# A convolution-attention layer followed by attention and experts: V projected behind the positional products, x loaded late, Q's first half in a written order

## Chip, core and metric

The kernel runs on one core of one Trainium2 chip, in one launch. The metric is the device time of the whole launch in microseconds (us), as the median of several runs. All arrays are float32. PE is TensorE (its weight loads are PEld), DVE is VectorE, ACT is ScalarE, POOL is GpSimd; SP is SyncE, from whose queue most transfers (DMAs) are issued.

## What is computed

The input x is 4 x 16 x 16 x 1024: 1024 positions ("tokens") in 4 images, 1024 channels. Layer 0 is the one that the change touches; cut to what matters it is

```python
xn = group_norm(x)                       # 32 groups of 32 channels, per image
q = bn(xn @ Wq, gamma, beta, mean, var)  # 1024 columns, 4 heads of 256
k = softmax(xn @ Wk)                     # 256 columns
v = bn(xn @ Wv, ...)                     # 256 columns
Lc = einsum("bkm,bvm->bkv", k, v)        # content
Yc = einsum("bhkn,bkv->bnhv", q, Lc)
Lp = einsum("nmk,bvm->bnkv", rel, v)     # relative positions
Yp = einsum("bhkn,bnkv->bnhv", q, Lp)
x = x + Yc + Yp
```

where bn(t) = (t - mean) * gamma / sqrt(var + 0.001) + beta. Layer 1, which the change leaves alone, is layer norm, multi-head attention with its projection, a second layer norm and eight gated experts, all added to x.

## The kernel before, in words

All tiles have 128 partitions. A float32 matmul runs as two passes, which the profile counts as two instructions. PSUM is held as eight banks: three under the tag mm, three under tr, and one tile of two banks under sc. The order of instructions on each engine, and of transfers on each queue, is not the program's order: a planner places an instruction when its inputs are ready in the planner's own picture of time, the earlier in the program first. Each engine and each queue then works strictly in that order, and an instruction whose semaphores are not there yet holds up those behind it.

**Loads (lines 178 to 209).** The tile xn receives x transposed, one chunk of 128 channels after the other, alternating with chunks of the first half of Wq; then come the second half of Wq, the four batch-norm rows of Q (tile q_rows), the positional table emb and, last, the eight tiles xs of x in its own layout (line 209). x is needed only where the result of layer 0 is added to it (line 429). Two large places called big0 and big1 (32 KB per partition each) are used in turn by many tiles: xn and then s0 use big0; q_rows, two_T and ln1 use big1. The eight xs tiles have a pool of their own. The two places of wpool hold, in turn, the two halves of Wq, w_kv, ln_rows and the two halves of w_v.

**Group norm and Q's first half (lines 214 to 295).** For each chunk c, group_means takes statistics on DVE and averages them over groups with a small matmul (pm); group_spreads does it for the variance (pv, line 233); group_norm takes the inverse root and lets ACT normalise the chunk in place, in four pieces. Six of the eight token tiles of Q's first half (the list early) are multiplied chunk by chunk as the chunks become ready, in six banks; the norms run two chunks ahead. batch_norms prepares scale and shift of V (vp) and Q (q_scale, q_shift); its reciprocal over 1024 columns is line 131, called from line 257. q_out (line 266) scales a bank into q_s (line 268), which frees the bank, and spreads it over q0 with four additions (line 272). The other ten token tiles follow one at a time in mm banks.

**K and V (lines 303 to 345).** K is projected and put through its softmax; then V in four groups of eight matmuls, each copied to v_T by ACT (line 339).

**Positional products (lines 366 to 402).** s0[m, n] sums, for every position n and head, what multiplies v at position m. The positional part is built in four groups R, with matmuls pT of windows of emb (copied by POOL, line 382, four buffers) and q0. The results of a group go to a half of two_T by ACT and DVE in turn (line 392). When a group is complete, its rows are moved to their partitions of s0 by transfers on SP's queue (line 399), 60 in all: 23, 22, 8 and 7 for R = 1, 2, 0 and 3. R = 0 reuses the half of R = 1, and R = 3 that of R = 2.

**Content and result (lines 347 and 410 to 432).** For each of eight token tiles, content adds the products of K and Q to s0 (line 361); the matmuls py multiply s0 by v_T (line 422); DVE adds the result to xs (line 429); layer_norm makes ln1 for layer 1; and x plus a bias is stored to x_rows (line 432), from which layer 1 reads it back at line 656.

Of the kernel before, what the change touches and what calls it, by code (L numbers as in the profile page):

```python
# [31 lines left out]
F32 = mybir.dt.float32  # L32
I32 = mybir.dt.int32
AF = mybir.ActivationFunctionType
ALU = mybir.AluOpType
# [3 lines left out]
P = 128  # L39
C = 1024  # L40
NC = C // P
B = 4
M = 256
TOK = B * M
NT = TOK // P
# [9 lines left out]
HALF = 512  # L55
BN_EPS = 0.001
# [9 lines left out]
def kernel(  # L66
# [27 lines left out]
    nc = tc.nc  # L94

    def pool(stack, name, bufs=1, **kw):
        return stack.enter_context(tc.tile_pool(name=name, bufs=bufs, reuse_waits="tile", **kw))
# [10 lines left out]
    def big_tile(n, name, shape=(NC, TOK)):  # L108
        return big[n].tile([P, *shape], F32, tag="big", name=name)
# [11 lines left out]
    def mm(name):  # L121
        return ps.tile([P, HALF], F32, tag="mm", name=name)
# [4 lines left out]
    def inverse_root(dst, var, eps):  # L127

        nc.vector.tensor_scalar(dst, var, eps, None, ALU.add)
        nc.scalar.activation(dst, dst, AF.Sqrt)  # L130
        nc.vector.reciprocal(dst, dst)
# [2 lines left out]
    make_identity(nc, ident)  # L134
    x_home = ExitStack()

    def tiles_of_x(name):
        xpool = pool(x_home, name, side="right")
        return [xpool.tile([P, C], F32, tag=f"x{t}", name=f"{name}{t}") for t in range(NT)]

    xs = tiles_of_x("x")
    dram = ctx.enter_context(tc.tile_pool(name="dram", bufs=1, space=bass.MemoryType.DRAM))
    x_rows = dram.tile([TOK, C], F32, name="x_rows")

# [30 lines left out]

    with ExitStack() as layer0:
        l0 = pool(layer0, "l0")
        xn = big_tile(0, "xn")
        w_q = [wpool.tile([P, NC, HALF], F32, tag="w", name=f"w_q{kc}") for kc in range(2)]
        for c in range(NC):  # L180
            nc.sync.dma_start(xn[:, c, :], xT[ts(c, P), :])
# [11 lines left out]
        with ExitStack() as projection:  # L193
# [8 lines left out]

            q_rows = big_tile(1, "q_rows", (NC, TOK))
            q_scale, q_shift, mean_q, var_q = (q_rows[:, i, :] for i in range(4))
            for t, a in ((q_scale, q_gamma), (q_shift, q_beta), (mean_q, q_mean), (var_q, q_var)):
                nc.sync.dma_start(t, a.partition_broadcast(P))
            nc.sync.dma_start(emb.rearrange("p c i j -> p c (i j)"), embT)
            for t in range(NT):
                nc.sync.dma_start(xs[t], x[ts(t, P), :])


            chunks = {}
# [1 line left out]
            def group_means(c):  # L214
                stats = small.tile([P, B, 6], F32, tag="gn_stats", name=f"gn_stats{c}")
                mv = small.tile([P, B, 2], F32, tag="gn_mv", name=f"gn_mv{c}")
                for b in range(B):
                    nc.vector.bn_stats(stats[:, b, :], xn[:, c, ts(b, M)])
                    nc.vector.bn_aggr(mv[:, b, :], stats[:, b, :])
                pm = tr(f"gn_pm{c}")  # L220
                nc.tensor.matmul(pm[:, :B], average, mv[:, :, 0], start=True, stop=True)
                chunks[c] = mv, pm
# [27 lines left out]


            def batch_norms():
                inverse_root(vp[:, 3, :], vp[:, 3, :], BN_EPS)
                nc.vector.tensor_mul(vp[:, 0, :], vp[:, 0, :], vp[:, 3, :])
                nc.vector.tensor_mul(vp[:, 2, :], vp[:, 2, :], vp[:, 0, :])
                nc.vector.tensor_sub(vp[:, 1, :], vp[:, 1, :], vp[:, 2, :])
                inverse_root(var_q, var_q, BN_EPS)
                nc.vector.tensor_mul(q_scale, q_scale, var_q)
                nc.vector.tensor_mul(mean_q, mean_q, q_scale)
                nc.vector.tensor_sub(q_shift, q_shift, mean_q)  # L260


            def q_product(pq, kc, t, c):
                nc.tensor.matmul(pq, xn[:, c, ts(t, P)], w_q[kc][:, c, :], start=(c == 0), stop=(c == NC - 1))  # L264
# [12 lines left out]

            two = ps.tile([P, 2, HALF], F32, tag="sc", name="pq_two", bufs=1)
            early = [mm(f"pq0_{t}") for t in range(3)] + [two[:, 0, :], two[:, 1, :], tr("pq0_5")]
            group_means(0)  # L280
            group_spreads(0)
            group_norm(0)
            group_means(1)
            group_spreads(1)
            group_norm(1)
            for c in range(NC):
                for t, pq in enumerate(early):
                    if c + 2 < NC and t in (1, 3):
                        (group_means if t == 1 else group_spreads)(c + 2)
                        if t == 3:  # L290
                            group_norm(c + 2)
                    q_product(pq, 0, t, c)
            batch_norms()
            for t, pq in enumerate(early):
                q_out(pq, 0, t)
            for kc in range(2):
# [27 lines left out]
                nc.vector.reciprocal(total, total)  # L324
                nc.vector.tensor_scalar(k_q[:, b, kc, :], k_e, total, None, ALU.mult)


            for j in range(2):
                for th in range(2):
                    pv = mm(f"pv{j}_{th}")  # L330
                    for c in range(NC):
                        nc.tensor.matmul(  # L332
                            pv,
                            w_kv[:, c, M + j * P : M + (j + 1) * P],
                            xn[:, c, ts(th, HALF)],
                            start=(c == 0),
                            stop=(c == NC - 1),
                        )
                    nc.scalar.activation(
                        v_T[:, j, ts(th, HALF)],  # L340
                        pv,
                        AF.Identity,
                        bias=vp[:, 1, j : j + 1],
                        scale=vp[:, 0, j : j + 1],
                    )

        def content(b, ih):

            heads = slice(b * HEADS0, b * HEADS0 + HEADS0)
# [17 lines left out]
        s0 = big_tile(0, "s0", (2, SIDE, SIDE, BH))  # L367
        tpool = pool(layer0, "tpool", 2)
        two_T = big_tile(1, "two_T", (2, SIDE, SIDE, BH))
        for n, (R, first, n_i) in enumerate(((1, 0, 16), (2, 0, 15), (0, 8, 8), (3, 0, 7))):  # L370
            rows = min(S2, REL - S2 * R)
            parts = rows * SIDE
            group = 2 if n_i > S2 else 4
            T = two_T[:, n % 2, :n_i, :, :]
            for n0 in range(0, SIDE, group):
                pT = mm(f"pT{R}_{n0}")
                out_T = pT[:parts, : group * BH * n_i].rearrange("p (j i h) -> p j i h", j=group, h=BH)
                for g in range(group):
                    nj = n0 + g
                    at = SIDE - 1 - nj  # L380
                    window = tpool.tile([P, 2, rows, SIDE], F32, tag="window", name=f"window{R}_{nj}", bufs=4, padded_shape=[P, 2, S2, SIDE])
                    nc.gpsimd.tensor_copy(window, emb[:, :, S2 * R : S2 * R + rows, at : at + SIDE])
                    for kc in range(2):
                        nc.tensor.matmul(
                            out_T[:, g, :, :],
                            window[:, kc, :, :].rearrange("p i j -> p (i j)"),
                            q0[:, kc, first : first + n_i, nj, :],
                            start=(kc == 0),
                            stop=(kc == 1),
                        )  # L390
                evict = nc.scalar.copy if n0 // group % 2 == 0 else nc.vector.tensor_copy
                evict(T[:parts, :, n0 : n0 + group, :].rearrange("p i j h -> p j i h"), out_T)
            for i in range(n_i):
                ni = first + i
                start = S2 * R + ni - SIDE + 1
                for mh in range(2):
                    lo, hi = max(start, mh * S2), min(start + rows, mh * S2 + S2)
                    if lo < hi:
                        nc.sync.dma_start(  # L399
                            s0[(lo - mh * S2) * SIDE : (hi - mh * S2) * SIDE, mh, ni, :, :],  # L400
                            T[(lo - start) * SIDE : (hi - start) * SIDE, i, :, :],
                        )

        ln1 = big_tile(1, "ln1")
        ln_rows = wpool.tile([P, 4, C], F32, tag="w", name="ln_rows")
        bp = ln_rows[:, 3, :]
        nc.gpsimd.dma_start(bp, b_proj.partition_broadcast(P))
        tiles = [(b, nt) for nt in (1, 0) for b in range(B)]  # L410
        for i, (b, nt) in enumerate(tiles):
            if i == 0:
                content(b, nt)
# [22 lines left out]
    with ExitStack() as attention:  # L436
# [212 lines left out]
        for i in range(len(steps) + 2):  # L649
            if i >= 2:  # L650
                s_T = turned(*steps[i - 2], soft.pop(i - 2))
            for unit in units.get(i, ()):
                project_qk(*unit)
            if i == 27:
                sums.close()
                xs = tiles_of_x("xb")
                for t in range(NT):
                    nc.sync.dma_start(xs[t], x_rows[ts(t, P), :])
            if i in out_at:
                project_out(*out_at[i])  # L660
            if i >= 2:
                values(*steps[i - 2], s_T)
            if i < len(steps):
                soft[i] = scores(*steps[i])
# [599 lines left out]
```

## Time and profile before

| what | value |
|---|---|
| median of 3 runs | 1316.14 us (1314.88 to 1316.62) |
| the profiled execution | 1314.95 us, of which the span from the first to the last instruction is 1313.2 us |
| mean granted PE clock | 0.996 |

Layer 0 by stretches, in us from the start of the span, with each engine's busy time:

| stretch | what PE works on | length | PE | DVE | ACT | POOL |
|---|---|---|---|---|---|---|
| 0 to 12.2 | first norms | 12.2 | 2.32 | 6.00 | 2.23 | 3.08 |
| 12.2 to 61.2 | Q, six early tiles | 49.0 | 47.41 | 29.87 | 19.71 | 0 |
| 61.2 to 129.9 | Q, the other ten | 68.7 | 68.70 | 41.15 | 0 | 0 |
| 129.9 to 157.8 | K | 27.9 | 27.90 | 9.67 | 3.96 | 1.97 |
| 157.8 to 185.4 | V | 27.6 | 27.60 | 0.94 | 2.90 | 0 |
| 185.4 to 230.5 | positional products | 45.1 | 41.89 | 7.40 | 8.78 | 23.76 |
| 230.5 to 303.7 | content, py, layer norm | 73.2 | 70.42 | 43.38 | 20.40 | 20.59 |
| 303.7 to 1313.2 | layer 1 | 1009.5 | 994.39 | 520.74 | 187.06 | 294.18 |

How to read the views. A line of the timeline gives start, duration, engine, source line, operation, the tile written and read, shapes and the number of merged instructions; in brackets stands how long the engine had been idle and what released it. A line of waits gives the waiting instruction, the one it waited for, the total, the number and the longest. PE's busy time includes matmuls that run at a lower granted clock, so slow matmuls are seen in the clock column and not as idle time.

### The profile page before, as it was taken

What the parts mean: (1) busy time and instruction counts of PE and PEld (TensorE: products, weight loads), DVE (VectorE), ACT (ScalarE), POOL (GpSimd) and SP (SyncE); (2) the same over time, 40 slices, a digit from 0 to 9 for tenths busy, and PEclk for the clock granted to TensorE, in tenths of its full rate; (3) what the DMA queues carried; (4) which work ended last, traced back from release to release, by engine and by line L of the source; (5) the groups of instructions that cost most, each with busy time, mean ns of one, the idle gap of its engine ahead of it and who ended that gap; (6) DMA issues with size and microseconds to landing.
All of it is one profiled execution on the core that took longest, in us unless ns stands there. A gap on an engine that the chain in (4) does not pass through costs nothing.

```text
span 1313.2 us, 12226 instructions
## 1 busy us (share of the span) xinstructions
PE 1280.6 (98%) x4506; PEld 690.6 (53%) x4506; DVE 659.1 (50%) x1248; ACT 245.0 (19%) x572; POOL 343.6 (26%) x365
## 2 busy tenths in 40 slices
PE   6999999999999999999999998999999999999998
PEld 3444858678884555555544544444444444444443
DVE  5674201567322555554435755664646465555642
ACT  3200111131000333333323322111111111111110
POOL 0000015131000111112111112455454544453530
PEclk9999999999999999999999998999999999999999
DMA  9320013212102202010405315284747566555542
GB/s 354 124 65 0 17 64 95 67 65 96 64 1 64 65 0 65 1 64 1 179 14 178 128 65 190 64 240 104 221 116 196 143 167 175 146 163 141 113 80 50
DMA packets 61040, 136.11 MB, mean 104 GB/s; under 512 B 5904, under 2 KB 20256, under 8 KB 60976
## 3 DMA queue, kind: packets, MB, share of 16 engines
q1 hardware_dynamic: 47664, 94.32, 20.6%
q0 software_dynamic: 13312, 40.96, 14.2%
q8 instruction: 37, 0.61, 0.2%
q14 instruction: 27, 0.22, 0.1%
HBM read 97.51 MB, written 33.55 MB: 100 GB/s over the span
## 4 chain that ended last, share of the span: by engine, by line
PE 91%; SPq 3%; DVE 2%; POOL 1%; issue 1%; DMA 1%; ACT 0%; DVEq 0%; ACTq 0%; POOLq 0%
PE p L1073 28%; PE pqk L470 15%; PE po L627 8%; PE pq L264 8%; PE pv L470 7%; PE one_pe L717 6%; SPq L399 3%; PE py L422 2%; PE pk L312 2%; PE pv L332 2%; PE sc L554 2%; PE pst L598 2%; PE pa L608 2%; PE pc L353 2%; PE pq_two L264 1%; POOL w_e_xg L696 1%
## 5 line engine op out<-in xcount | busy, mean ns | idle before, releaser
L696 POOL DMA_INDIRECT w_e_xg<-rows,gather x152 | 160.3, 1054 | 69.5 <-issue 41.8
L1073 PE MATMUL p<-w_e,A 128*128 128x512 f32 x368 | 162.9, 592 | 1.8 <-DVE slot L934 1.8
L586 POOL TENSOR_TENSOR s<-s,total 128x256 f32<-128x256 f32 x64 | 51.6, 827 | 341.1 <-DVE total L583 341.1
L1073 PEld LDWEIGHTS p<-w_e,A 128*128 128x128 f32 x368 | 69.8, 190 | 89.4 <-issue 88.0
L627 PE MATMUL po<-w_p,y_T 128*128 128x512 f32 x256 | 116.1, 598 | 0.0
L1073 PE MATMUL p<-T,S 128*128 128x512 f32 x256 | 112.7, 592 | 0.0
L724 POOL DMA_INDIRECT out_dram<-y,add x32 | 58.8, 1838 | 204.5 <-ACT y L1079 134.8
L1079 ACT ACTIVATE y<-y,slot 128x512 f32<-128x512 f32 x64 | 46.2, 722 | 340.1 <-DVE y L1087 166.4
L264 PE MATMUL pq<-w_q,xn 128*128 128x512 f32 x224 | 102.1, 608 | 1.6 <-ACT xn L243 1.6
L470 PE MATMUL pqk<-ln,w_qk 128*128 128x512 f32 x192 | 85.0, 592 | 0.0
L717 PE MATMUL one_pe<-w_e,one 128*128 128x512 f32 x192 | 83.4, 592 | 0.0
L1073 PEld LDWEIGHTS p<-T,S 128*128 128x128 f32 x256 | 48.6, 190 | 60.8 <-issue 60.7
L627 PEld LDWEIGHTS po<-w_p,y_T 128*128 128x128 f32 x256 | 46.3, 190 | 49.1 <-issue 48.7
L264 PEld LDWEIGHTS pq<-w_q,xn 128*128 128x128 f32 x224 | 42.7, 194 | 52.0 <-issue 48.9
L706 DVE STREAM_TRANSPOSE A<-w_e_xg 128x1024 f32<-128x1024 f32 x32 | 39.7, 1241 | 42.7 <-DMA w_e_xg<-rows,gather 42.6
L717 PEld LDWEIGHTS one_pe<-w_e,one 128*128 128x128 f32 x192 | 36.5, 190 | 45.9 <-issue 45.9
L576 ACT ACTIVATE s<-s,top 128x256 f32<-128x256 f32 (+1 forms) x128 | 56.6, 443 | 17.7 <-DVE top L574 17.7
L470 PEld LDWEIGHTS pqk<-ln,w_qk 128*128 128x128 f32 x192 | 35.9, 190 | 42.1 <-issue 41.1
L470 PE MATMUL pqk<-T,S_qk 128*128 128x512 f32 x128 | 57.7, 593 | 0.0
L1073 PE MATMUL p<-w_e,S 128*128 128x512 f32 x128 | 57.5, 592 | 0.0
L1073 PE MATMUL p<-T,A 128*128 128x512 f32 x128 | 57.5, 592 | 0.0
L599 ACT COPY s_T<-pst 128x384 f32<-128x384 f32 x64 | 27.5, 481 | 157.9 <-PE pst L598 157.9
(253 smaller groups left out, 1784.8 us busy)
## 6 DMA issues: line engine op xcount, KB each, us to landing
w_e<-in_expert_w_dram SPq DMA_DIRECT2D x16, 2048.0 KB, 11.4
w_qk<-in_W_attnT_dram SPq DMA_DIRECT2D x8, 1024.0 KB, 6.4
xn<-in_xT_dram SPq DMA_DIRECT2D x8, 512.0 KB, 8.1
x<-in_x_dram SPq DMA_DIRECT2D x8, 512.0 KB, 11.3
w_v<-in_W_attnT_dram SPq DMA_DIRECT2D x2, 2048.0 KB, 8.2
x_rows<-x SPq DMA_DIRECT2D x8, 512.0 KB, 2.6
w_p<-in_W_projT_dram SPq DMA_DIRECT2D x2, 2048.0 KB, 7.6
xb<-x_rows SPq DMA_DIRECT2D x8, 512.0 KB, 7.6
```

Source lines behind the costliest of these rows:

```text
L264: nc.tensor.matmul(pq, xn[:, c, ts(t, P)], w_q[kc][:, c, :], start=(c == 0), stop=(c == NC - 1))
L399: nc.sync.dma_start(s0[(lo - mh * S2) * SIDE : (hi - mh * S2) * SIDE, mh, ni, :, :], T[(lo - start) * SIDE : (hi - start) * SIDE, i, :, :],)
L470: nc.tensor.matmul(bank, stationary(c), moving(c), start=(c == 0), stop=(c == NC // 2 - 1))
L576: nc.scalar.activation(s[:, h, cols], s[:, h, cols], AF.Exp, bias=top[:, qt, h : h + 1], accum_out=total[:, qt, h : h + 1],)
L586: nc.gpsimd.tensor_mul(s[:, :, cols], s[:, :, cols], total[:, qt, :].unsqueeze(2).to_broadcast([P, 2, (qt + 1) * P]),)
L627: nc.tensor.matmul(po, y_T[:, c, ts(t, P)], w_p[j][:, c, :], start=(c == 0), stop=(c == NC - 1))
L696: nc.gpsimd.indirect_dma_start(out=row[:, g, :], out_offset=None, in_=table[: (TOK - P) * Q, :] if e in SHORT else table, in_offset=bass.I ...
L706: nc.vector.transpose(row_T.rearrange("p c (g j) -> p g c j", g=Q), row.rearrange("p g (c i) -> p g c i", c=NC),)
L717: nc.tensor.matmul(pe, row_T[:, c, :], w[j][:, c, :], start=(c == 0), stop=(c == NC - 1))
L724: nc.gpsimd.indirect_dma_start(out=out[: TOK - P, :] if e in SHORT else out, out_offset=bass.IndirectOffsetOnAxis(ap=add[:, e, k : k + 1], ...
L1073: nc.tensor.matmul(bank, a[:, c, :], b[:, c, :], start=(c == 0), stop=(c == NC // 2 - 1))
L1079: nc.scalar.mul(y[i][:, ts(j, HALF)], y[i][:, ts(j, HALF)], slot[:, e, 1, 2 * pair + i : 2 * pair + i + 1])
```

## The change

1. **Places.** xn moves from big0 to a pool x_pool; s0 then has big0 to itself. x is no longer loaded at the start: a tile x_at of the same tag as xn, so in the same place, is loaded behind V's projection, in the order in which the tiles are used.
2. **V behind the positional products.** The loop of V's four groups stands behind the loop of the groups R and ahead of the loads of x.
3. **Places in two_T.** R = 3 writes rows 8 to 14 of the first half, so it reuses a part of what R = 1 held; R = 0 keeps rows 0 to 7 of it.
4. **Q's first half in a written order.** Within manual_schedule each engine issues its instructions in the order of the program; where they fall among instructions outside the block stays the planner's. The norms run one chunk ahead instead of two. keep_warm issues matmuls whose result is overwritten: 14 ahead of the first means, 3 and 5 in the steps behind. The inverse root of Q's variance is taken in pieces: root after chunk 4, a quarter of the reciprocal after chunks 5 and 6 each, the last half after the loop; Q's scale then stands ahead of V's in batch_norms. The row var_q is the first of the four to be loaded.

```diff
-    xs = tiles_of_x("x")
+    x_pool = pool(x_home, "x_pool", side="right")
...
-        xn = big_tile(0, "xn")
+        xn = x_pool.tile([P, NC, TOK], F32, tag="x", name="xn")
...
-            for t, a in ((q_scale, q_gamma), (q_shift, q_beta), (mean_q, q_mean), (var_q, q_var)):
+            for t, a in ((var_q, q_var), (q_scale, q_gamma), (mean_q, q_mean), (q_shift, q_beta)):
                 nc.sync.dma_start(t, a.partition_broadcast(P))
             nc.sync.dma_start(emb.rearrange("p c i j -> p c (i j)"), embT)
-            for t in range(NT):
-                nc.sync.dma_start(xs[t], x[ts(t, P), :])
...
             def batch_norms():
+                nc.vector.tensor_mul(q_scale, q_scale, var_q)
+                nc.vector.tensor_mul(mean_q, mean_q, q_scale)
+                nc.vector.tensor_sub(q_shift, q_shift, mean_q)
                 inverse_root(vp[:, 3, :], vp[:, 3, :], BN_EPS)
...
-                inverse_root(var_q, var_q, BN_EPS)
-                nc.vector.tensor_mul(q_scale, q_scale, var_q)
-                nc.vector.tensor_mul(mean_q, mean_q, q_scale)
-                nc.vector.tensor_sub(q_shift, q_shift, mean_q)
...
-            group_means(0)
-            group_spreads(0)
-            group_norm(0)
-            group_means(1)
-            group_spreads(1)
-            group_norm(1)
-            for c in range(NC):
-                for t, pq in enumerate(early):
-                    if c + 2 < NC and t in (1, 3):
-                        (group_means if t == 1 else group_spreads)(c + 2)
-                        if t == 3:
-                            group_norm(c + 2)
-                    q_product(pq, 0, t, c)
-            batch_norms()
+
+            def keep_warm(n):
+                for _ in range(n):
+                    nc.tensor.matmul(early[0][:, :P], average, average, start=True, stop=True)
+
+            with tc.manual_schedule():
+                keep_warm(14)
+                group_means(0)
+                keep_warm(3)
+                group_spreads(0)
+                keep_warm(5)
+                group_norm(0)
+                for c in range(NC):
+                    for t, pq in enumerate(early):
+                        q_product(pq, 0, t, c)
+                        if t == 1 and c + 1 < NC:
+                            group_means(c + 1)
+                        elif t == (3 if c == 0 else 2) and c + 1 < NC:
+                            group_spreads(c + 1)
+                            group_norm(c + 1)
+                    if c == NC - 4:
+                        nc.vector.tensor_scalar(var_q, var_q, BN_EPS, None, ALU.add)
+                        nc.scalar.activation(var_q, var_q, AF.Sqrt)
+                    elif NC - 4 < c < NC - 1:
+                        n = c - (NC - 3)
+                        nc.vector.reciprocal(var_q[:, ts(n, M)], var_q[:, ts(n, M)])
+                nc.vector.reciprocal(var_q[:, HALF:], var_q[:, HALF:])
+                batch_norms()
...
-        for n, (R, first, n_i) in enumerate(((1, 0, 16), (2, 0, 15), (0, 8, 8), (3, 0, 7))):
+        for R, first, n_i, T in (
+            (1, 0, 16, two_T[:, 0, :, :, :]),
+            (2, 0, 15, two_T[:, 1, :15, :, :]),
+            (0, 8, 8, two_T[:, 0, :8, :, :]),
+            (3, 0, 7, two_T[:, 0, 8:15, :, :]),
+        ):
...
-            T = two_T[:, n % 2, :n_i, :, :]
...
+        x_at = x_pool.tile([P, NT, C], F32, tag="x", name="x_at")
+        xs = [x_at[:, t, :] for t in range(NT)]
+        tiles = [(b, nt) for nt in (1, 0) for b in range(B)]
+        for b, nt in tiles:
+            t = 2 * b + nt
+            nc.sync.dma_start(xs[t], x[ts(t, P), :])
```

The loop of V is moved unchanged from behind K to just ahead of these last lines. At the read-back of x in layer 1 only names change.

## The prediction

> **What bounds the kernel now.** First the page: busy shares, then the forty slices.
>
> ```profile
> PE 1280.6 (98%) x4506; PEld 690.6 (53%) x4506; DVE 659.1 (50%) x1248; ACT 245.0 (19%) x572; POOL 343.6 (26%) x365
> PE   6999999999999999999999998999999999999998
> ```
>
> TensorE (PE) is busy for 98% of the span; the chain that ended last puts 91% on it. So the end moves only by PE's idle time (1313.2 - 1280.6 = 32.6 us) and by matmuls that run slow. Everything on other engines counts only if PE waits for it. The second view is the list of PE's waits.
>
> ```profile
> PE gn_pm L221 <- DVE gn_mv L219: 7.7, 2, 6.4
> PE pT L384 <- ACT two_T L392: 3.2, 1, 3.2
> PE gn_pv L233 <- DVE gn_spread L231: 2.2, 2, 1.1
> PE pq L264 <- ACT xn L243: 1.6, 1, 1.6
> PE py L422 <- DMA s<-two_T: 1.4, 1, 1.4
> ```
>
> The columns are total, times, longest. These five lie in layer 0, the only part whose work changes. The third view, stretches of the span (PE, PEld, DVE, ACT, POOL busy, granted clock, DMA), shows what follows the 3.2 us wait.
>
> ```profile
> 225.00:226.00 1.00, 0.00 (x0) 0.00 (x0) 0.00 (x0) 0.00 (x0) 0.00 (x0) 1.00 0.39 114
> 227.00:228.00 1.00, 0.63 (x3) 0.66 (x4) 0.38 (x1) 0.98 (x3) 0.00 (x0) 0.51 0.47 138
> 229.00:230.00 1.00, 1.00 (x7) 1.00 (x7) 0.00 (x0) 0.00 (x0) 0.00 (x0) 0.50 0.41 100
> 231.00:232.00 1.00, 1.00 (x4) 0.47 (x3) 0.33 (x1) 0.00 (x0) 0.00 (x0) 1.00 0.20 50
> ```
>
> PE's idle is followed by half clock until about 230.7. The fourth view, the timeline, names the causes.
>
> ```profile
> 12.21 2.07 PE L264 MATMUL pq<-w_q,xn 128*128 128x512 f32 x2
> 42.94 6.55 DVE L131 RECIPROCAL q_rows<-q_rows 128x1024 f32<-128x1024 f32 x1 [0.84 <-ACT q_rows L130]
> 57.09 0.69 DVE L268 TENSOR_TENSOR q_s<-pq,q_rows 128x512 f32<-128x512 f32 x1 [1.85 <-PE pq L264]
> 200.12 15.12 SPq L399 DMA_DIRECT2D s<-two_T  x22
> 214.65 26.06 SPq L399 DMA_DIRECT2D s<-two_T  x39
> 227.37 3.25 PE L384 MATMUL pT<-q,window 128*112 128x112 f32 x16 [3.21 <-ACT two_T L392]
> 238.90 3.90 PE L422 MATMUL py<-v_T,s 128*128 128x256 f32 x16 [1.41 <-DMA s<-two_T]
> ```
>
> Q starts at 12.21. One 6.55 us reciprocal on VectorE (DVE) delays chunk 7's group norm. The 60 transfers of the positional products leave SP at 0.68 us each, 200.12 to 240.7, and outlast the products; the last group and then py wait for them.
>
> **What the Trainium skill says.** "TensorE: Matmul & The Clock Gate", Part 1 (The HAM clock gate): half clock until one free-running activity window of about 3.4 us has been busy, and again after an idle one. The trace agrees roughly: Q's matmuls are slow from 12.21 to about 18.5, and here 3.2 us of idle already sufficed. "DMA: Bandwidth & Descriptors", Anatomy of one DMA: a semaphore wait is held by the issuing sequencer, not by the DMA engines. It agrees: in SP's own waits the load of w_v stood 101.4 us until V's last matmul; whatever follows on SP stands behind it. "VectorE: DVE Perf Modes", the walkthrough's fixed hardware budget: a reciprocal iterates eight times. It agrees: 6.55 us for 1024 columns beside 1.23 for a multiply.
>
> **Part 1, values behind the positional products.** V's 64 matmuls (157.78 to 185.35, 27.6 us) are moved, not removed. The four groups then follow K directly. From the rows: first start 185.35, last group interrupted at 224.16 with 48 of its 64 matmuls done, so 38.8 us; the other 16 at the full-clock pitch of 0.097 us take 1.6 instead of the 3.2 of idle and 3.25 slow. Group R=3 gets its own place in two_T (rows 8 to 14 of the first half): it waits for R=1's transfers, not R=2's. R=1's 23 leave from 14.8 us after the start of the products (200.12 - 185.35) and end 15.6 later, landed at about 32.5; R=3's first copy is due after 13.8 + 12.9 + 6.8 = 33.5, plus its first products. No wait. **Gain 4.8 us** (3.2 + 3.25 - 1.6).
>
> All 60 transfers have left SP by 14.8 + 60 x 0.68 = 55.6; the products (40.4) and V (27.6) keep PE until 68.0. So 12 us of cover, and py's wait goes: **1.4 us**. Without that cover the 1.4 remains. s0 in a place that xn never held frees nothing else: in the kernel before its first transfer came well after V anyway. V's four ScalarE (ACT) copies of 0.78 us move with it; the last ends 0.8 us into the content products (7.0 us), before py reads v_T, and the 1.28 us table load for the layer norm's roots (227.67 before) then has 12 us to spare. On POOL the windows keep their place behind the bias load that waits for Q's last weights (130.31); four are ready at 134.7, before K ends. On SP the s0 transfers pass w_v's first half, which now stands behind them. Sum of part 1: **6.2 us**.
>
> **Part 2, x late.** Eight loads of 512 KB leave SP's first burst (nothing waited for their absence: Q runs on chunks landed long before) and wait for V's last matmul. Behind them on SP stand w_v's first half (not needed for 63 us: V ends 230.45 in this trace's terms, project_v starts 293.38) and the x_rows stores. First need of x: py's add, which in this trace comes 10.6 us after the products' end (241.06 - 230.45), 9.2 without the DMA wait. The first xn load, the same size, landed 3.9 us after issue; in a row of eight the median of x was 11.3. From below the cost is nothing, as the first tile is due at 9.2, the second 5.3 later (246.32), the rest 7.8 apart, and tile k lands at about 3.9 + 1.3k; from above 11.3 - 9.2 = 2.1 us once. A gain is excluded: nobody waited for x. I take **0**.
>
> **Part 3, Q's order.** Warm matmuls: 14 of 128 columns, two passes each. At half clock a pass of 512 is 0.85 us (estimate from 12 to 18), so of 128 0.21: 14 take 6.0 from about 1.6, at full clock half. Means(0) is ready at 6.44. Full clock for the second half gives no delay, all cold 1.2 us. The groups of 3 and 5 (0.6 and 1.1 us at full clock) fit into the two steps behind. The chain behind: means to spreads 0.8, spreads to the first normalised quarter 1.45 (35.42 to 36.9 in chunk 5), no statistics of chunk 1 between. First product at 9.3 (early clock) to 10.6 (late): I take 9.9, and full clock from there.
>
> A chunk costs 5.60 (22.15 to 27.75: six products of 0.86, two norm pairs). With one product, 0.86, between means and spreads instead of two, and 0.77 of DVE plus latencies, add 0.17 for six chunks; the reciprocal of a quarter (6.55/4 = 1.7) in front of chunk 7's statistics adds 0.3. The early block ends at 9.9 + 7 x 5.6 + 1.0 + 0.3 + 5.2 = 55.6; now 61.2.
>
> But the next group needs a bank that the first q_out frees, and DVE is late. Chunk 7's norm leaves DVE at 48.7; quarter 1.7, half 3.3, two multiplies of 1.23: 56.2. If the planner slips the first q_out multiply (0.69) in there, which the code's fixed order allows since q_out stands outside it, the bank is free at 57.0; after the subtraction and the first step of V's scale at 58.4; behind all of V's scale (about 1.4 with its trip through ACT) at 59.7. Now it starts at 61.2. Gains 4.2, 2.8, 1.5; the third has 4.1 us of idle and so half clock after it, minus 1.65 (half of 3.3, as at 227 to 230.7), leaving -0.1. I take the middle, **2.8**; bounds -0.1 and 4.2. Afterwards q_out's 3.1 us per tile stays under PE's 6.87.
>
> **Sum.** 6.2 + 0 + 2.8 = 9.0. The profiled execution took 1314.95 (span 1313.2 and 1.75 around it), so 1305.9; it lies 1.2 under the median 1316.14, so 1307.
>
> **Rivals.** *A stall takes the place of the norm's wait:* the written batch_norms hold DVE, PE idles 4 us and clocks down; part 3 gives about 0, total 6.2, 1310. For it: 6.55 us of reciprocal plus 3.7 of multiplies must still run, now after chunk 7's norm. Chance 0.22. *x late for the add:* 2.1 us, total 6.9, 1309.2; for it speaks only the median of a crowded queue; 0.12. *Slower, SP's order:* if the planner, whose order on SP put w_v ahead of all s0 transfers before, puts x's loads in front of n of them, those leave only after V, 0.68 us each. Eight loads at about 0.5 and landing of 2 make py late by 6 + 0.68n - 7; at 9 us (n above 15) all is lost. With all 37 of R=2, 0 and 3, 24 us, or 1316 + 24 - 9 = 1331. Against it: they are written first and ready 12 us earlier. Chance 0.08. That the change doesn't take hold: the places and queues are written, so no separate case.
>
> **Numbers.** Forecast 0.58 at 1307 (own range 1304.6 to 1309). What this kernel's measurement can tell from no change is 0.2%, 2.6 us. Faster: 0.58 + 0.12 + 0.18 of the stall case's 0.22, together 0.88; within 0.2%: the other 0.04 of it, where the sizes are smaller still; slower 0.08. Range: from 11 us gained (1304) to the stall case with 1.5 more (1311.5).
>
> **What would show it.** Right: no PE wait of pT for ACT two_T and of py for the DMA; clock 1.00 from 215 to 235; Q's first product near 10; the bank wait of pq for DVE q_s of 1 to 3 us. Wrong: SP's x loads standing between s0 transfers, DVE x waiting for DMA x, or half clock after the early block.

## The result, and the profile after

The changed kernel takes 1310.25 us (median of 5 runs, 1307.83 to 1311.38) against 1316.14: a ratio of 0.9954, 95% interval 0.9939 to 0.997. That is 5.9 us faster; 9 were forecast. Its profiled span is 1308.4 us, against 1313.2. Of all runs reported below one, of half_scale, was in a slow state (2734.52 us), and its ratio leaves it out.

The page's busy shares and PE's forty slices, for the changed kernel:

```profile
PE 1286.6 (98%) x4550; PEld 695.5 (53%) x4550; DVE 664.3 (51%) x1250; ACT 245.3 (19%) x572; POOL 344.3 (26%) x365
...
PE   9999999998999999999999998999999999999998
...
PEclk9999999998999999999999998999999999999999
```

PE has no more idle at the start; but one slice, the tenth, which was full before, now has both idle time and a lower clock. PE's waits say which (total, times, longest):

```profile
PE row_pt L818 <- DVE row L836: 4.9, 2, 3.7
PE pv L489 <- DVE T L478: 3.5, 1, 3.5
PE p L1093 <- DVE slot L954: 1.8, 1, 1.8
PE pq L276 <- DVE average L195: 1.6, 1, 1.6
...
PE pq L257 <- DVE q_s L261: 1.1, 1, 1.1
PE pn L1015 <- DVE U L1105: 1.0, 1, 1.0
PE pq L257 <- ACT xn L237: 0.3, 1, 0.3
PE gn_pm L215 <- DVE gn_mv L213: 0.3, 1, 0.3
```

Gone are the waits of pT for the copy and of py for the transfers, 4.6 us together, and almost all of those of the group norms. New are 1.1 us for the bank that the first q_out frees, and 3.5 us in layer 1, where V's second products wait for the sum T. That wait was there before, at 1.0 (L276 is the warming's own start):

```profile
PE pv L470 <- DVE T L459: 1.0, 1, 1.0
```

The timeline of the changed kernel, at the places that were shown of the kernel before:

```profile
9.78 1.98 PE L257 MATMUL pq<-w_q,xn 128*128 128x512 f32 x4 [0.32 <-ACT xn L237]
50.49 3.29 DVE L299 RECIPROCAL q_rows<-q_rows 128x512 f32<-128x512 f32 x1
56.22 0.68 DVE L261 TENSOR_TENSOR q_s<-pq,q_rows 128x512 f32<-128x512 f32 x1
...
171.11 29.02 SPq L391 DMA_DIRECT2D s<-two_T  x44
...
199.54 11.19 SPq L391 DMA_DIRECT2D s<-two_T  x17
...
224.23 3.82 SPq L422 DMA_DIRECT2D x_at<-in_x_dram  x8
228.32 3.71 PE L441 MATMUL py<-v_T,s 128*128 128x256 f32 x16
```

Q starts at 9.78 at full clock (four instructions in 1.98 us, where two took 2.07 before). The s0 transfers leave SP by 210.7, while V's matmuls run until 224; x's loads follow them. So py starts at 228.32 instead of 238.90: at this point the changed kernel is 10.6 us ahead. The ends of the two spans are only 4.8 us apart. V now stands where the transfers run, and PE is full there at full clock (start and end of the stretch, its length, then the busy time of PE, PEld, DVE, ACT and POOL, granted clock, DMA's share, GB/s):

```profile
196.00:224.20 28.20, 28.20 (x73) 12.89 (x72) 1.22 (x2) 2.33 (x3) 0.00 (x0) 1.00 0.23 63
```

The starts of the same work in both profiles show where the lead goes:

| work | before | after | after is ahead by |
|---|---|---|---|
| K | 129.94 | 125.82 | 4.1 |
| first py | 238.90 | 228.32 | 10.6 |
| layer 1, V's first products without a wait | 303.68 | 292.89 | 10.8 |
| layer 1, first product of Q and K | 394.89 | 389.37 | 5.5 |
| experts, first product behind PE's wait for the slot list | 843.30 | 837.10 | 6.2 |
| its end, first expert bias product | 874.44 | 869.94 | 4.5 |

Two places cost it: 5.3 us in layer 1's V, and 1.7 at the start of the experts; in between, 0.7 us come back. At the second, the same eight instructions take longer, first before, then after:

```profile
843.30 3.67 PE L1073 MATMUL p<-w_e,A 128*128 128x512 f32 x8 [1.82 <-DVE slot L934]
837.10 5.37 PE L1093 MATMUL p<-w_e,A 128*128 128x512 f32 x8 [1.82 <-DVE slot L954]
```

The first place, in the timeline of the changed kernel:

```profile
294.86 1.27 SPq L117 DMA_DIRECT2D w_v<-in_W_attnT_dram  x1
294.89 0.42 DVE L511 TENSOR_TENSOR v<-pv,v 128x256 f32<-128x256 f32 x1 [4.31 <-PE pv L489]
298.26 2.29 DVE L477 TENSOR_TENSOR T<-ln 128x2048 f32<-128x2048 f32 x1 [2.95 <-DMA x_rows<-x_at]
...
303.47 5.49 PE L489 MATMUL pv<-s_v,T 128*128 128x256 f32 x12 [3.51 <-DVE T L478]
```

DVE's first sum T waits 2.95 us for a store of x to x_rows, although it reads only ln1. PE waits for T, and then works at half clock (columns as in the stretch above):

```profile
303.40:309.00 5.60, 5.53 (x13) 4.46 (x14) 5.60 (x6) 0.00 (x0) 0.00 (x0) 0.50 0.00 0
309.00:315.00 6.00, 6.00 (x29) 5.26 (x29) 3.27 (x6) 0.00 (x0) 0.00 (x0) 0.99 0.00 0
```

Thirteen matmuls in the first 5.6 us, 29 in the next 6. The kernel before had full clock at this place, twelve in 2.86 us:

```profile
311.74 2.86 PE L470 MATMUL pv<-s_v,T 128*128 128x256 f32 x12 [0.99 <-DVE T L459]
```

So 2.5 us more of wait (3.51 against 0.99) and 2.75 of half clock (the 384 matmuls from there take 85.90 us on the chain that ended last, against 83.15 before).

### The profile page after: what moved, and what is told of

Same layout as the page of the kernel before. It is cut to its first block, busy times and chain, and to the rows that moved or that the text cites. A ratio compares the mean times of both kernels' runs of the same rounds, so it can differ in the third digit from the quotient of the medians.

```text
span 1308.4 us, 12324 instructions
## 1 busy us (share of the span) xinstructions
PE 1286.6 (98%) x4550; PEld 695.5 (53%) x4550; DVE 664.3 (51%) x1250; ACT 245.3 (19%) x572; POOL 344.3 (26%) x365
## 4 chain that ended last, share of the span: by engine, by line
PE 93%; DVE 4%; POOL 1%; DMA 1%; issue 1%; ACT 0%; DVEq 0%; ACTq 0%; POOLq 0%
PE p L1093 28%; PE pqk L489 15%; PE po L646 8%; PE pq L257 7%; PE pv L489 7%; PE one_pe L737 6%; PE pT L376 3%; PE py L441 2%; PE pk L319 2%; PE pc L340 2%; PE pv L401 2%; PE sc L573 2%; PE pst L617 2%; PE pa L627 2%; PE last_pe L1209 1%; POOL w_e_xg L716 1%
## 5 line engine op out<-in xcount | busy, mean ns | idle before, releaser
L646 PEld LDWEIGHTS po<-w_p,y_T 128*128 128x128 f32 x256 | 46.3, 190 | 49.1 <-issue 48.7
L618 ACT COPY s_T<-pst 128x384 f32<-128x384 f32 x64 | 27.5, 481 | 157.6 <-PE pst L617 157.6
```

The lines of the kernel that those rows point to most:

```text
L646: nc.tensor.matmul(po, y_T[:, c, ts(t, P)], w_p[j][:, c, :], start=(c == 0), stop=(c == NC - 1))
```

## The experiments

The theory formed on this profile: T lies where x lay, and as the change holds x in one tile, T waits for the last user of all of x, the eighth store; before, with eight tiles, it did not. The rivals: the later load of w_v or the later stores do it, whatever the tiles are. The kernels were timed in three groups: sep_x, old_place, v_first and old_q; after_again, no_warm, half_scale and early_sums; T_left and sep_sums. Each ratio is to the kernel before as timed in the same group (medians 1315.61, 1316.29 and 1315.79 us). All times are medians, of 4 to 22 runs each. after_again is the changed kernel once more; its first five runs and these six together have a median of 1309.61 us, with which the others are compared below. As most kernels stand in another group than these eleven runs, differences of about 1 us between medians mean little.

**Eight tiles instead of one (sep_x).**

```diff
-        xn = x_pool.tile([P, NC, TOK], F32, tag="x", name="xn")
+        xn = [x_pool.tile([P, TOK], F32, tag=f"x{c}", name=f"xn{c}") for c in range(NC)]
...
-        x_at = x_pool.tile([P, NT, C], F32, tag="x", name="x_at")
-        xs = [x_at[:, t, :] for t in range(NT)]
+        xs = [x_pool.tile([P, C], F32, tag=f"x{t}", name=f"x{t}") for t in range(NT)]
```

> The change, with xn held as eight tiles of one chunk each and x as eight tiles in their places, instead of one tile each. Theory (one tile): the first of layer 1's sums T overlaps x's place and, with x in one tile, waits for the last of the eight x_rows stores; eight tiles make it wait only for those it overlaps. Then PE's wait pv for DVE T falls from 3.5 us to about 1.0 and the half clock after it goes: 5.3 us less than the change, about 1305. Rival (the loss is the later load of w_v or the later stores, not the tile): PE's wait stays at 3 us or more and the time at 1310. Instruction order on DVE is that of the change.

Measured: 1304.12 us, ratio to the kernel before 0.9915 (0.9902 to 0.9928). In its profile DVE goes from the add to the sum without a wait:

```profile
295.14 0.42 DVE L510 TENSOR_TENSOR v<-pv,v 128x256 f32<-128x256 f32 x1 [4.31 <-PE pv L488]
295.48 2.28 DVE L476 TENSOR_TENSOR T<-ln 128x2048 f32<-128x2048 f32 x1
...
301.20 2.86 PE L488 MATMUL pv<-s_v,T 128*128 128x256 f32 x12 [0.99 <-DVE T L477]
```

Twelve matmuls now take 2.86 us, not 5.49. The time is 5.5 us below 1309.61, as the theory had it. But the eight tiles also change something else: their places come free one by one, so x's loads leave SP from 218.48 on, ahead of V's end, and not from 224.23.

**T elsewhere (T_left).** To see that it is the shared place and not the earlier loads, x stays in one tile and T is taken from the other end of the memory:

```diff
-        s_pool = pool(sums, "s_pool", 2, side="right")
+        s_pool = pool(sums, "s_pool", 2)
```

> The change, x in one tile as it has it, but the pool of layer 1's sums T taken from the other end of the memory, where x does not lie. Theory (T waits because it lies on x's one tile): PE's wait pv for DVE T falls to about 1.0 us here too, without a change to x: 1304 to 1305, as with the eight tiles. Rival (the eight tiles helped in another way, by earlier loads or stores of x): the wait stays above 3 us, 1309 to 1310.

Measured: 1303.79 us, 0.9907 (0.9892 to 0.9921). PE's waits in its profile:

```profile
PE pv L489 <- DVE T L478: 1.2, 1, 1.2
```

The same gain by another way, 5.8 us, and x's loads leave SP at 224.58, as in the change. The rival falls.

**R = 3 in its old place (old_place).**

```diff
-            (3, 0, 7, two_T[:, 0, 8:15, :, :]),
+            (3, 0, 7, two_T[:, 1, :7, :, :]),
```

> The change, but group R = 3 of the positional products reuses the half of two_T that R = 2 held, as before. Theory: its first copy waits for R = 2's transfers again, PE idles about 3.2 us and works 3.3 us at half clock, so 4.8 us more than the change, about 1315; py does not wait, as V's matmuls cover the transfers. Rival (with V behind it the stall is covered too): 1310, no wait of pT.

Measured: 1313.32 us, 0.9985 (0.9978 to 0.9992), 3.7 us more than the changed kernel. The timeline has the stall, with V's matmuls behind it:

```profile
198.98 3.30 PE L376 MATMUL pT<-q,window 128*112 128x112 f32 x16 [3.31 <-ACT two_T L384]
202.07 4.50 PE L401 MATMUL pv<-xn,w_kv 128*128 128x512 f32 x7
```

V starts 5.0 us later than in the changed kernel (202.28 against 196.71 on the two chains, less 0.5, by which K started later: 126.42 against 125.89), near the 4.8 that was expected. The half clock then runs on into V, whose first seven instructions take 4.50 us. V behind the products does not cover this stall: PE's order is fixed, and V waits behind pT. The two profiled runs lie 4.8 us apart (1315.03 against 1310.25); the medians lie closer, as the profiled run of old_place was one of its slower ones.

**V ahead of the products (v_first).** The loop of V is moved back to ahead of the products; nothing else is.

> The change, but V's matmuls stand ahead of the positional products, as before; R = 3's own place and the late x stay. Theory (the transfers' issue on SP is the bound): products end 40.4 us after their start, but the transfers that the first tiles need leave SP by 14.8 + 53 x 0.67 = 50 and land at 52; content products cover 6.9, so py waits about 5 us and works some us at half clock: 5 to 7 us more than the change, 1315 to 1317: R = 3's place alone moves the stall from pT to py and gains nothing. Rival (the two gains of my prediction are separate): only py's wait of 1.4 us returns, 1311.7.

Measured: 1315.9 us, 1.0003 (0.9994 to 1.0012), 6.3 more than the changed kernel and the time of the kernel before.

```profile
221.69 7.04 PE L360 MATMUL pc<-q,k_q 128*128 128x512 f32 x16
234.94 5.37 PE L441 MATMUL py<-v_T,s 128*128 128x256 f32 x16 [6.21 <-DMA s<-two_T]
```

The products run through, and then py waits 6.2 us, 1 us more than worked out, and is slow (16 in 5.37 us, against 3.71). R = 3's place without V behind it gains nothing: the 60 issues on SP, not the place, were the bound, and V's 27.5 us cover them. From the start of K to the first py the profiles have:

| kernel | K | first py | between |
|---|---|---|---|
| before | 129.94 | 238.90 | 108.96 |
| old_place (V behind, old place) | 126.35 | 235.17 | 108.82 |
| v_first (own place, V ahead) | 126.07 | 234.94 | 108.87 |
| the change (both) | 125.82 | 228.32 | 102.50 |

So the two edits of part 1 are no sum of 4.8 and 1.4. Each alone gains 0.1 us: the one leaves the stall at pT, the other moves it to py.

**Q in the planner's order (old_q).** The block from keep_warm to batch_norms and the order of the four rows are those of the kernel before.

> The change without its part 4: Q's first half, batch norms and the order of their rows as in the kernel before. Theory: K starts 4.1 us later, as in the two profiles (129.94 against 125.82), so 1314.4; nothing behind K changes. Rival (the planner's order behind the block differs too, or the gain of the block is hidden by a later wait): 1310 to 1312.

Measured: 1312.59 us, 0.9973 (0.9964 to 0.9981), 3.0 more than the changed kernel, between the theory's 1314.4 and the rival's 1312. K starts at 129.91 on its chain that ended last, against 125.89 on that of the changed kernel, 4.0 later, as expected; the median shows less. Its profile also shows that the half clock behind T's wait is not sure to come: PE waits 3.2 us there, and the 384 matmuls behind take 83.15 us, at full clock.

**The changed kernel once more (after_again).**

> The change itself, once more, beside the next three on one chip, for its place in the same comparison and for a second profile. Theory (the half clock after layer 1's T wait comes in some executions only): the wait stays at 3.2 to 3.9 us in its profile, with 384 matmuls of V behind it taking 83 us at full clock or 86 with half clock at their start; median 1309 to 1311.

Measured: 1308.99 us, 0.9931 (0.9914 to 0.9948). T's wait is 3.8 us, and the matmuls behind take 85.65 us: half clock again. Over six profiles with a wait of 3.1 to 3.9 us at this place (this kernel twice, no_warm, old_place, v_first, old_q), the 384 matmuls took 85.90, 85.65, 86.08, 84.71, 83.15 and 83.15 us; with 1.0 to 1.2 us of wait (before, sep_x, half_scale, T_left) always 83.15.

**No warming (no_warm).** keep_warm returns without a matmul.

> The change without its 22 warming matmuls. Theory (full clock is granted after 3 to 7 us of work): Q's first product starts no earlier (9.8, it hangs on the statistics) but runs at half clock for 3.4 to 6.8 us, so K starts 1.7 to 3.4 us later than the 125.8 of the change, which is 1312 to 1313.6. Rival (DVE's chain of reciprocals sets the start of the seventh token tile anyway, so the warm start is hidden): K at the same time, 1310, and the bank wait for DVE q_s shorter by as much.

Measured: 1313.45 us, 0.9965 (0.995 to 0.998), 3.8 us more than the changed kernel. Its timeline:

```profile
10.34 3.78 PE L257 MATMUL pq<-w_q,xn 128*128 128x512 f32 x4 [1.53 <-ACT xn L237]
...
14.20 1.48 PE L257 MATMUL pq<-w_q,xn 128*128 128x512 f32 x2
```

Four instructions take 3.78 us, not 1.98: the pace of half clock until about 14.7, although the clock column reads 1.00 there, as it does for the slow start of the kernel before; so this column doesn't show the slow start. K comes at 128.74 on the chain, 2.9 later than in the changed kernel's first profile and 2.6 later than in its second. The bank wait for q_s stays at 1.1: DVE's chain hangs on the norms, so it comes later by as much and hides nothing. The rival falls. Of the 2.9 us, 0.6 are a later first product: 0.2 of it a later landing of x's first chunk (its statistics start at 4.51 against 4.34), the rest lies in the steps behind, where the two small matmuls are slow too (0.59 us each, not 0.39).

**Q's scale by halves (half_scale),** on sep_x: scale and shift of the first 512 columns ahead of the last reciprocal.

```diff
+                q_rows_of(0)
+                for t, pq in enumerate(early[:3]):
+                    q_out(pq, 0, t)
                 nc.vector.reciprocal(var_q[:, HALF:], var_q[:, HALF:])
+                q_rows_of(1)
                 batch_norms()
```

> The eight-tile version (sep_x), with Q's scale and shift made for the first 512 columns ahead of the last reciprocal, and the first three q_out between. Theory: the bank wait of 1.1 us (PE pq for DVE q_s) goes, K starts about 1.1 us earlier, 1303. Rival (the wait is PE's own, or DVE falls behind later): K as in sep_x, 1304.

Measured: 1304.91 us, 0.9901 (0.9881 to 0.992): not faster than sep_x. The timeline shows where the 1.1 us went:

```profile
55.56 10.89 PE L261 MATMUL pq<-w_q,xn 128*128 128x512 f32 x25
...
63.30 3.35 DVE L306 RECIPROCAL q_rows<-q_rows 128x512 f32<-128x512 f32 x1
...
78.00 8.42 PE L261 MATMUL pq<-w_q,xn 128*128 128x512 f32 x19 [0.82 <-DVE q_s L265]
```

The seventh tile no longer waits, but the reciprocal now stands between the q_outs and a later tile waits 0.8 us for its bank. K starts at 126.33 against 126.16 in sep_x. The wait was moved; the 0.3 us by which it shrank don't show, as this profile's first product came 0.5 us later (10.52 against 10.03).

**The sums T earlier (early_sums, sep_sums).** On half_scale, and on sep_x, the first two sums stand in the program ahead of the adds of V's second products:

```diff
+            if r == 0:
+                first_sums_of_B()
             for t in range(4):
                 c11, c12, c21, c22 = homes(t)
                 nc.scalar.copy(c22, one(t, 1, a11, b11))
```

> half_scale, with the first two of layer 1's sums T emitted ahead of the adds of V's second products. Theory: what is left of PE's wait for DVE T (1.0 us) shrinks to 0.2, another 0.8 us: 1302. Rival (the adds pushed back hold PSUM banks and PE waits for them): no gain, 1303 or more.

> The eight-tile version (sep_x) with the first two sums T emitted ahead of the second products' adds, and Q's scale as in the change. Theory (half_scale gained nothing, as its bank wait came back as one of 0.8 us later; the order of the sums gained 0.9): K as in sep_x, PE's wait for DVE T gone, 1303. Rival (the two edits gain only together): 1304 or more.

Measured: early_sums 1302.57 us, 0.9887 (0.9868 to 0.9906); sep_sums 1303.77, 0.9907 (0.9891 to 0.9923). In both profiles PE's wait for T is gone, and the work behind it starts at 300.49 and 300.44, 0.9 and 0.8 ahead of half_scale and sep_x. sep_sums missed its 1303, and its median is only 0.35 us below that of sep_x, within the scatter of its own runs (1302.58 to 1304.97): that the earlier sums shorten the whole time is not shown by this pair. Whether the 1.2 us between early_sums and sep_sums are Q's halves or chance stays open: K starts at 126.27 and 126.23, and the profile of early_sums has the experts' start at full clock, sep_sums' not. Both beat the kernel before by 12 to 14 us and the changed one by 6 to 7.

## Why the prediction was right, and where it was not

**Part 1 (6.2 us): right in its sum, not in its split.** From the start of K to the first py the change gains 6.5 us. No wait of pT, none of py, and 13.4 us of wait on SP between its last s0 transfer and V's end, where 12 of cover were worked out. It priced R = 3's place at 4.8 on its own and said that without V's cover only the 1.4 us of py's wait would remain. v_first shows 6.2 us of wait there, with half clock behind it: each edit is worth nothing without the other.

**Part 2 (0): right at x's first use; beyond it, the step that failed.** DVE's adds of py wait for PE alone (8.3 us, as before), and x's loads leave SP behind all 60 transfers; the rivals of a late x and of SP's order did not come. But the step asked only who needs x first. It left out who needs x's place next. One tile where eight had been gives its place free only with its last store, and layer 1's T waited 2.5 us more for it, with 2.75 us of half clock in this profile behind. sep_x and T_left, two edits that share nothing but this, both take it back: 5.5 and 5.8 us. This is the whole difference between 9.0 and the measured 5.9, and more.

**Part 3 (2.8): right in its mechanism, too small.** It gave 4.1, the first of its three cases: the planner put the first q_out multiply behind two of Q's row products, at 56.22. The working before it was near: first product 9.9 predicted, 9.78 measured; chunk 5.77 against 5.75; chunk 7's norm leaving DVE at 48.7 against 48.9; end of the early block 55.6 against 55.8; bank free at 57.0 against 56.9. The mis-sized term is the choice among the three places in DVE's order: it took the middle one, 1.4 us behind the first. The trace of before spoke for the first: there too the planner had put other work between dependent row products (49.53 to 53.28), and the prediction did not use it. The stall rival, PE idle for 4 us, did not come: 1.1 us. Of the 4.1 us, no_warm gives 2.6 to 2.9 to the warming; how the rest divides between the order of the norms and the pieces of the reciprocal, no run shows. One reading in the prediction is loose: 6.55 us beside 1.23 is a factor of 5.3, which does not by itself confirm eight iterations.

**The sum** was thus 1.6 us too small for layer 0 (10.6 against 9.0) and had no entry for layer 1. The 1.7 us at the experts is no effect of the change that these runs can show: it is half clock behind waits of 0.6 to 1.7 and 1.8 us, seen in ten of the twelve profiles here and not in those of before and early_sums. That 1310.25 lies inside the stated range, 1304 to 1311.5, is in part luck: the slow end of the range was there for the stall behind Q, which did not come, and two errors of opposite sign met, a gain too small in layer 0 and a loss left out in layer 1.

**When a wait brings half clock.** The same 3.1 to 3.9 us of wait for T cost between 0 and 2.9 us of slow matmuls. The clock columns of the twelve profiles show what differs. In them half clock lasts 3.41 or 6.83 us, once or twice 3.41, each of the 29 times that it ends within the span, and within one profile its starts lie whole multiples of 3.413 us apart: in the changed kernel 302.25 and 838.14, 157 times. So each span, from 12 to 1300 us, can be cut into windows of this length on its profile's own grid. After a full-clock window with PE busy for 1.45 us or less, half clock followed each time (23 of 23); after one with 1.47 to 1.59 us in 6 of 10; after one with 1.69 us or more never (4430). In the changed kernel the wait for T left 1.12 us of work in one window. In v_first it was as long, but fell across two, with 1.76 and 1.49 us of work, and the clock stayed full. The experts' start is alike: the emptiest window there held 0.73 to 1.59 us of work in the ten profiles with half clock, and 1.59 and 1.79 in before and early_sums. The grid lay differently in every profile. This is a reading of the traces; no edit tested it.

The Trainium skill, "TensorE: Matmul & The Clock Gate", Part 1, gives about 3.4 us of idle for half clock, in a window that runs freely. The traces agree on the length and on the free running. They differ on the idle: a window need not be empty, as 1.45 us of work in it did not keep the clock.

## What to carry to other kernels

When a buffer takes over another's place, ask three questions and not one: who needs it first, who uses it last, and who is waiting for the place after that; merging several tiles into one makes the next owner wait for the last user of all. A wait that an edit removes may stand again one step later, when the bound is a queue's issue rate: price the queue to its end, and find work to cover all of it. And a wait of 3 us on PE costs its length and, where it empties one of the clock's windows, almost as much again in half clock; price it as a range.

## What was not expected of the hardware

The reciprocal on DVE costs 6.4 to 6.8 ns for each column (6.55 us for 1024, 3.29 for 512, 1.74 for 256), over five times a multiply of two tensors (1.22 us for 1024). The half clock also comes from waits that are much shorter than 3 us each: at the start of the experts two waits, of 0.6 to 1.7 and of 1.8 us, with two tiny matmuls between, were enough in ten of twelve profiles (8 instructions in 5.37 us instead of 3.67). And the warming matmuls do not give the same start each time: the first 28 instructions took 5.15 us in the changed kernel's profile and 6.07 in half_scale's. There they also held up the means, whose matmul came at 7.48 although its input was ready at 6.94, and Q's first product came at 10.52 instead of 9.78.
